# Row sums of four heads in one pass of TensorE, their quotients spread through DRAM, and two batches of x on chip instead of three

## The chip, the cores and the metric

The kernel runs on one NeuronCore of one Trainium2 chip. The metric is the device time of one execution in microseconds (us). Five engines work side by side, each through its own queue and in order: PE (TensorE) does matmuls, DVE (VectorE), ACT (ScalarE) and POOL (GpSimd) do elementwise work, SP (SyncE) issues the DMAs. SBUF is the on-chip memory with 128 partitions; matmuls write into PSUM. Everything is computed in float32.

## The reference, cut to what matters

x has 4 batches of 512 channels and 32 x 32 = 1024 positions. Four layers follow each other: softmax attention with 8 heads of 64 channels (layer 0), a linear attention (layer 1), softmax attention with one head of 512 (layer 2), and softmax attention with 4 heads of 128 (layer 3). The change is in layers 0 and 3, where each head does this:

```python
qkv = (xs @ Wp.T + bp).reshape(B, s, N_HEADS, 3 * D_K)
q, k, v = jnp.split(qkv, 3, axis=-1)
attn = jnp.einsum('bihd,bjhd->bijh', q, k) * SCALE
attn = jax.nn.softmax(attn, axis=2)
res = jnp.einsum('bijh,bjhd->bihd', attn, v)
...
out = res @ Wo.T + bo + xs
```

A softmax is a sum of exps over the keys for each query (the row sum), and a division by it. The kernel multiplies exp(scores) with v first, and divides the result.

## The kernel before, in words

`plain_path` is the program that runs (`general_path` is a fallback that this data doesn't take). Its loops run over the batches, layer by layer. PE's order is written out by hand (`manual_schedule` for PE); the order on the other engines comes from a planner that works with priorities and estimates. `later` holds work of PE that is due after a number of ticks (`tick`, once per step of attention or at chosen places of the projections); `pieces` holds parts of the next layer's work that fill `slot`s.

`attention` (L892) works on one batch. Queries are taken in two blocks qb of 512. The channels lie in four chunks g of 128: in layer 0 (`pair`) a chunk holds two heads of 64, in layer 3 one head. A step is (qb, g, i): in layer 0, i counts eight groups of 128 keys; in layer 3, four groups of 256 keys.

- `scores` (L908): PE multiplies keys with queries into a two-bank PSUM tile, four 64x64 matmuls that use the quarters of the array in layer 0, two full ones in layer 3. ACT takes the exp (L922) into one of four buffers `pt`, and DVE adds the pt of a chunk into `sum` (L926, L929), of which there are two buffers. In layer 3 a last add (L931) folds the two halves.
- `values` (L933), two steps behind: PE multiplies v with pt and accumulates over the keys into PSUM, one tile in layer 3, two (lower and upper half of the keys) in layer 0. There are four such tiles (`acc`). In layer 0, ACT copies the lower one to `ot` (L951) and DVE adds the upper one (L952).
- `sum_rows` (L961), once for each (qb, g): PE multiplies a matrix of ones with `sum`. This adds over the partitions and at once writes the total to every partition that needs it: one full matmul in layer 3 (L976), four on quarters of the array in layer 0 (L968), where ACT (L973) and DVE (L974) join two results. Then `invert` (L673) takes reciprocals on DVE (L675) and two maxima (L677, L678) for a test of the range at the end.
- `normalise` (L980): DVE multiplies the values with the reciprocals (L985), and ACT adds a bias to x (L988).
- `project_out` (L996), after the last chunk of a block: a first part and three further ones (`second`, `third`, `fourth`), with matmuls at L1018 and DVE adds at L1026 and L1048. They are due 2*per, and 2*per + 1, 2, 3 ticks later in layer 0 (per = 2), and 2*per and 2*per + 1, 1, 2 in layer 3 (per = 1).

So PE computes 32 units of row sums in layer 0 and 32 in layer 3. The tile `ot` is a single buffer.

x of a batch is 2 MB, 16 KB in each partition. Three of the four batches are on chip at a time (`x_tile`, L564). `away` (L568) stores a batch to DRAM and `back` (L572) fetches one. At the start batches 1 and 2 are loaded (L593); batch 3 follows when batch 0 has gone (L1596).

Of the kernel before, what the change touches and what calls it, by code (L numbers as in the profile page):

```python
# [13 lines left out]
F32 = mybir.dt.float32  # L14
AF = mybir.ActivationFunctionType
# [3 lines left out]
P = 128  # L19
B = 4  # L20
# [454 lines left out]
def plain_path(ctx: ExitStack, tc: tile.TileContext, d: dict, out: bass.AP, count):  # L475
# [35 lines left out]
    def sum_tile(name):  # L511
        return work.tile([P, 2, TB], F32, tag="sum", bufs=2, name=name)

    def v_tiles():

        return [work.tile([P, 2, C], F32, tag=f"v{i}", name=f"v{i}") for i in range(NT // 2)]
# [5 lines left out]
    def chunks_tile(tag, name, bufs=1):  # L522
        return work.tile([P, NC, TB], F32, tag=tag, bufs=bufs, name=name)
# [38 lines left out]
    xs, homes = {}, {}  # L562

    def x_tile(b):  # L564
        xs[b] = xpool.tile([P, NC, S], F32, tag="x", bufs=B - 1, name=f"x{b}")
        return xs[b]

    def away(b):  # L568
# [3 lines left out]
    def back(b):  # L572
        nc.sync.dma_start(x_tile(b), homes.pop(b))
# [15 lines left out]
    nc.sync.dma_start(wqkv0[:, :, 2 * C :], wview[:, :, 2 * C :])  # L589
    loaded0 = load_bias(d["bv0"], d["wo0n"], v_tiles()[:2])  # L590
    wo0 = load_wo(d["wo0"])
    for b in range(1, B - 1):
        nc.sync.dma_start(x_tile(b), xin[b])  # L593


    wv1 = chunks_tile("xn", "wv1", 2)
# [19 lines left out]
    nc.vector.memset(eps, 1e-5)  # L616
    UNITS = B * NTB * (NC + 1 + NC)
    tops = const.tile([P, 2, UNITS], F32, name="tops")
    unit = itertools.count()

    gmat = const.tile([P, P // GROUP, GROUP], F32, name="gmat")
# [51 lines left out]
    def invert(rd, ps):  # L673

        nc.vector.reciprocal(rd, ps)  # L675
        n = next(unit)
        nc.vector.tensor_reduce(tops[:, 0, n : n + 1], ps, AX.X, ALU.max)  # L677
        closing[:] = [nc.vector.tensor_reduce(tops[:, 1, n : n + 1], rd, AX.X, ALU.max).ins]  # L678

    def sum_inputs(tiles, inputs):  # L680

# [210 lines left out]
    def attention(b, q, key, v, heads, scale, wo, os, bo, hooks={}, last=False, end=None, plain=False):  # L892
# [12 lines left out]
        pts, accs, rds, outs, ots, exps = {}, {}, {}, {}, {}, []  # L905
        half = lambda i: slice(i * P // 2, (i + 1) * P // 2)

        def scores(n):  # L908
            qb, g, i = steps[n]
            ps = two_tile("sc")  # L910
            if pair:
                for h, s in itertools.product(range(2), range(2)):
                    nc.tensor.matmul(  # L913
                        ps[half(h), s, :], lhsT=key(g, i)[half(s), half(h)],
                        rhs=q[qb][half(s), g, :], start=True, stop=True,
                    )
# [5 lines left out]
            exps.append(nc.scalar.activation(pt, ps, AF.Exp, scale=scale).ins)  # L922
            pts[n] = pt
            if i == 1:
                accs[qb, g] = acc = sum_tile("sum")
                nc.vector.tensor_tensor(acc, pts[n - 1], pt, ALU.add)  # L926
            elif i > 1:
                acc = accs[qb, g]
                nc.vector.tensor_tensor(acc, acc, pt, ALU.add)  # L929
            if i == nsteps - 1 and not pair:  # L930
                nc.vector.tensor_tensor(acc[:, 0, :], acc[:, 0, :], acc[:, 1, :], ALU.add)  # L931

        def values(n):  # L933
            qb, g, i = steps[n]
            pt = pts.pop(n)
            if i == 0:
                outs[qb, g] = [acc_tile() for _ in range(2 if pair else 1)]
            if pair:

                for s, r in itertools.product(range(2), range(2)):  # L940
                    nc.tensor.matmul(  # L941
                        outs[qb, g][r][half(s), :],
                        lhsT=v[i // 2][half(r), i % 2, g * P + s * hd : g * P + (s + 1) * hd],
                        rhs=pt[half(r), s, :], start=(i == 0), stop=(i == NT - 1),
                    )
                if i == NT - 1:
                    if g == 0:
                        ots[qb] = chunks_tile("ot", "ot")
                    lower, upper = outs.pop((qb, g))
                    o = ots[qb][:, g, :]  # L950
                    nc.scalar.copy(o, lower)  # L951
                    nc.vector.tensor_tensor(o, o, upper, ALU.add)  # L952
                return
            for s in range(2):
                j = 2 * i + s
                nc.tensor.matmul(  # L956
                    outs[qb, g][0], lhsT=v[j // 2][:, j % 2, bass.ts(g, P)], rhs=pt[:, s, :],
                    start=(j == 0), stop=(j == NT - 1),
                )

        def sum_rows(qb, g):  # L961

# [14 lines left out]
            rds[qb, g] = row_tile("rd")  # L977
            invert(rds[qb, g], ps)

        def normalise(qb, g):  # L980
            rd = rds.pop((qb, g))
            if g == 0 and not pair:
                ots[qb] = chunks_tile("ot", "ot")
            o = ots[qb][:, g, :]
            nc.vector.tensor_tensor(o, o if pair else outs.pop((qb, g))[0], rd, ALU.mult)  # L985
# [111 lines left out]
        for m in range(0, len(steps) + 2, per):  # L1097
            for n in range(m, m + per):
                if n < len(steps):
                    scores(n)  # L1100
            for n in range(m, m + per):
                if n >= 2:
                    qb, g, i = steps[n - 2]
                    final = i == nsteps - 1

                    if final and not pair:
                        sum_rows(qb, g)
                    values(n - 2)
                    tick()
                    if final and pair:  # L1110
                        later.append([1, lambda qb=qb, g=g: (sum_rows(qb, g), normalise(qb, g))])
                    elif final:
                        normalise(qb, g)
                    if n - 2 == len(steps) - 1 and end is not None:
                        flush()
                        end_program(qb)
                    elif final and g == NC - 1 and plain and qb == NTB - 1:
                        later.append([2 * per + 1, lambda qb=qb: project_out_plain(qb)])
                    elif final and g == NC - 1:
                        rest = []  # L1120
# [344 lines left out]

    def layer_norm(b, tb, tiles):

        x = xs[b][:, :, bass.ts(tb, TB)]
        t = {}

        def add():
            s = t["s"] = row_tile("s")
            nc.vector.tensor_tensor(s, x[:, 0, :], x[:, 1, :], ALU.add)
            for c in range(2, NC):
                nc.vector.tensor_tensor(s, s, x[:, c, :], ALU.add)

        def center():
            xn = tiles[tb]
            t["ps"] = two_tile("lnsums")
            mean = t["ps"][:, 0, :]  # L1480
            nc.tensor.matmul(mean, lhsT=ones, rhs=t["s"], start=True, stop=True)
            for c in range(NC):
                nc.vector.scalar_tensor_tensor(
                    xn[:, c, :], mean, -1.0 / C, x[:, c, :], ALU.mult, ALU.add
                )
# [75 lines left out]

    def verdict():

        assert next(unit) == UNITS
# [9 lines left out]
    with tc.manual_schedule(engines={mybir.EngineType.PE}):  # L1574
# [8 lines left out]
        for b in range(B):  # L1583
# [86 lines left out]
        for b in range(B):  # L1670
# [73 lines left out]
        for b in range(B):  # L1744
# [92 lines left out]
```

## Time and profile before

| | |
|---|---|
| runs (3) | median 2488.96 us, 2487.82 to 2489.7 |
| the profiled execution | 2487.56 us, its span (first to last instruction) 2485.8 us |
| granted TensorE clock | 0.999 of full speed |
| busy | PE 2468.6 us (99%), DVE 1679.0 (68%), ACT 705.0 (28%), POOL 253.6 (10%) |
| layer 0, attention of batch 0 (80 to 212 us) | PE 130.75 us of 132.00, DVE 117.24, ACT 75.71 |
| layer 3, attention of batch 0 (1697 to 1825 us) | PE 128.00 us of 128.00, DVE 86.20, ACT 41.06 |
| DMA | 72.47 MB, mean 29 GB/s |

In a row of a group of instructions stand the line, the engine, the operation, output<-inputs, for PE the rows and columns of the array in use (64*64), the shape, the count, and then busy us, the mean ns of one, and the idle time of the engine before it with what ended it. A float32 matmul shows as two records. Records of PE overlap[...]; what a matmul costs is the time from its start to the next start. A row of waits gives the waiting engine, tile and line, what it waited for, the us in total, the times, and the longest. Rows of a timeline give start and length in us. A row of DMA issues gives the tile, the count, the KB of each and the median time from issue to landing.

### The profile page before, as it was taken

Reading aid. Unit: us, or ns where it says so; the run is one execution under the profiler, and the core shown is the slowest. Engines: PE = TensorE matmul, PEld = TensorE weight load, DVE = VectorE, ACT = ScalarE, POOL = GpSimd, SP = SyncE. Lnnn points to the kernel's source line nnn. Section 1 sums busy time; section 2 is a strip of 40 time slices with the busy share of each in tenths; the row PEclk is TensorE's granted clock in tenths of the full one; section 3 lists DMA queues with packets and bytes.
Section 4 is the critical chain, followed back from the end, with each engine's and each line's share of the span. In section 5 each row is a group of like instructions: output and inputs, shape, how many; then the busy total and the mean of one; then the engine's idle time right before and its main releaser. Section 6 shows DMA issues by size and latency. Waiting matters only on the chain.

```text
span 2485.8 us, 24942 instructions
## 1 busy us (share of the span) xinstructions
PE 2468.6 (99%) x10218; PEld 1277.3 (51%) x10218; DVE 1679.0 (68%) x1941; ACT 705.0 (28%) x863; POOL 253.6 (10%) x240
## 2 busy tenths in 40 slices
PE   9999999999999999999999999999999999999999
PEld 4545544554455444544645546445556446555653
DVE  3788588858875888647486775755664773665465
ACT  1454154315531544221211201112211320321121
POOL 4001100110011001201203021021010001002000
PEclk9999999999999999999999999999999999999999
DMA  5000010001000301010101010110010000000000
GB/s 216 1 1 1 5 69 1 1 5 69 1 1 5 119 10 51 0 72 9 59 0 68 5 67 19 51 68 17 17 51 1 5 13 17 1 17 17 1 9 27
DMA packets 23304, 72.47 MB, mean 29 GB/s; under 512 B 1808, under 2 KB 9488, under 8 KB 21136
## 3 DMA queue, kind: packets, MB, share of 16 engines
q1 hardware_dynamic: 23184, 70.82, 7.8%
q8 instruction: 82, 1.34, 0.2%
q14 instruction: 38, 0.31, 0.0%
HBM read 44.60 MB, written 25.17 MB: 28 GB/s over the span
## 4 chain that ended last, share of the span: by engine, by line
PE 96%; DVE 3%; issue 1%; ACT 0%; DMA 0%; SPq 0%; DVEq 0%
PE acc L703 20%; PE acc L824 11%; PE sc L918 9%; PE acc L956 9%; PE sc L913 8%; PE acc L941 8%; PE acc L831 8%; PE acc L1018 6%; PE acc L1232 6%; PE acc L1193 2%; PE acc L968 1%; PE acc L976 1%; PE feat L638 1%; DVE sum L929 1%; PE acc L638 1%; DVE rd L675 1%
## 5 line engine op out<-in xcount | busy, mean ns | idle before, releaser
L922 ACT ACTIVATE pt<-sc 128x1024 f32<-128x1024 f32 x384 | 380.3, 1022 | 650.4 <-PE sc L918 391.5
L929 DVE TENSOR_TENSOR sum<-sum,pt 128x1024 f32<-128x1024 f32 x256 | 313.9, 1226 | 45.8 <-ACT pt L922 34.4
L941 PE MATMUL acc<-pt,v 64*64 64x512 f32 x2048 | 291.0, 590 | 0.0
L913 PE MATMUL sc<-q,k 64*64 64x512 f32 x2048 | 273.7, 591 | 1.1 <-ACT pt L922 1.1
L956 PE MATMUL acc<-pt,v 128*128 128x512 f32 x512 | 239.9, 592 | 0.0
L918 PE MATMUL sc<-q,k 128*128 128x512 f32 x512 | 239.8, 593 | 0.0
L675 DVE RECIPROCAL rd<-acc 128x512 f32<-128x512 f32 x32 | 107.4, 3357 | 107.0 <-PE acc L976 107.0
L691 POOL TENSOR_TENSOR ws<-wqkv 128x256 f32<-128x256 f32 (+1 forms) x40 | 40.6, 1015 | 1334.8 <-PE acc L968 552.3
L703 PE MATMUL acc<-t,ws 128*128 128x512 f32 x384 | 173.9, 593 | 0.0
L941 PEld LDWEIGHTS acc<-pt,v 64*64 64x64 f32 x2048 | 104.2, 133 | 121.3 <-issue 98.3
L913 PEld LDWEIGHTS sc<-q,k 64*64 64x64 f32 x2048 | 101.1, 133 | 123.6 <-issue 92.4
L956 PEld LDWEIGHTS acc<-pt,v 128*128 128x128 f32 x512 | 97.3, 190 | 122.5 <-issue 120.5
L918 PEld LDWEIGHTS sc<-q,k 128*128 128x128 f32 x512 | 96.8, 190 | 112.8 <-issue 88.1
L703 PEld LDWEIGHTS acc<-t,ws 128*128 128x128 f32 x384 | 72.5, 190 | 86.6 <-issue 85.1
L675 DVE RECIPROCAL rd<-rs 128x512 f32<-128x512 f32 x32 | 107.3, 3352 | 1.1
L926 DVE TENSOR_TENSOR sum<-pt 128x1024 f32<-128x1024 f32 x64 | 76.7, 1198 | 42.1 <-ACT pt L922 42.1
L742 ACT COPY v<-acc 128x512 f32<-128x512 f32 x24 | 14.0, 585 | 287.9 <-PE acc L824 287.9
L824 PE MATMUL acc<-ws,t 128*128 128x256 f32 x384 | 87.3, 379 | 0.0
L831 PE MATMUL acc<-qs,w 128*128 128x512 f32 x192 | 86.6, 593 | 0.0
L831 PE MATMUL acc<-q,ln 128*128 128x512 f32 x192 | 85.8, 593 | 0.0
L733 DVE TENSOR_TENSOR v<-acc,v 128x512 f32<-128x512 f32 x72 | 49.4, 688 | 51.9 <-PE acc L824 51.7
L742 ACT COPY q<-acc 128x512 f32<-128x512 f32 x40 | 23.4, 585 | 207.8 <-PE acc L703 207.8
(318 smaller groups left out, 3698.2 us busy)
## 6 DMA issues: line engine op xcount, KB each, us to landing
home<-x SPq DMA_DIRECT2D x8, 2048.0 KB, 6.3
x<-home SPq DMA_DIRECT2D x8, 2048.0 KB, 7.8
out<-x SPq DMA_DIRECT2D x32, 256.0 KB, 2.1
x<-in_x SPq DMA_DIRECT2D x3, 2048.0 KB, 16.9
wo<-in_wo SPq DMA_DIRECT2D x3, 1024.0 KB, 5.3
w<-in_w SPq DMA_DIRECT2D x1, 3072.0 KB, 17.8
wqkv<-in_wqkv SPq DMA_DIRECT2D x1, 3072.0 KB, 10.1
wqkv<-in_wqkv SPq DMA_DIRECT2D x2, 1024.0 KB, 9.2
```

The costliest lines, as they stand in the source:

```text
L675: nc.vector.reciprocal(rd, ps)
L703: nc.tensor.matmul(ps, lhsT=w[:, m, :], rhs=x[:, m, :], start=start, stop=stop, skip_group_check=True)
L824: nc.tensor.matmul(ps[:, bass.ts(r, C // 2)], lhsT=x[:, m, bass.ts(2 * o + r, P)], rhs=w[:, m, :], start=(start and r == 0), stop=stop, sk ...
L831: nc.tensor.matmul(ps, lhsT=x[:, m, bass.ts(o, P)], rhs=w[:, m, :], start=start, stop=stop, skip_group_check=True,)
L913: nc.tensor.matmul(ps[half(h), s, :], lhsT=key(g, i)[half(s), half(h)], rhs=q[qb][half(s), g, :], start=True, stop=True,)
L918: nc.tensor.matmul(ps[:, s, :], lhsT=key(g, 2 * i + s), rhs=q[qb][:, g, :], start=True, stop=True)
L922: exps.append(nc.scalar.activation(pt, ps, AF.Exp, scale=scale).ins)
L929: nc.vector.tensor_tensor(acc, acc, pt, ALU.add)
L941: nc.tensor.matmul(outs[qb, g][r][half(s), :], lhsT=v[i // 2][half(r), i % 2, g * P + s * hd : g * P + (s + 1) * hd], rhs=pt[half(r), s, : ...
L956: nc.tensor.matmul(outs[qb, g][0], lhsT=v[j // 2][:, j % 2, bass.ts(g, P)], rhs=pt[:, s, :], start=(j == 0), stop=(j == NT - 1),)
L1018: nc.tensor.matmul(ps[i][:, bass.ts(o, n)], lhsT=w[:, m, bass.ts(o, P)], rhs=t[:, m, :], start=(start and m + o == 0), stop=(stop and m == ...
L1232: nc.tensor.matmul(ps[i, o], lhsT=w[m][:, bass.ts(o, P)], rhs=t[m], start=(start and m == 0), stop=(stop and m == 3), skip_group_check=True,)
```

## The change

In layer 0 the row sums of two chunks (four heads) become one unit, except for the last two chunks of the second query block, which stay with `sum_rows`. In layer 3 the four heads of the first query block, and the first three of the second, become one unit each; the last head stays with `sum_rows`. A unit (`sum_shared`) multiplies ones of 32 columns with each head's sum, and writes head k to partitions 32k to 32k + 31 of one PSUM tile. One `invert` serves the unit. As the reciprocals of a head are then on 32 partitions only, one row of each head is stored to DRAM, and loaded back broadcast to the partitions that need it; `normalise` of all chunks of the unit follows that. In layer 3, ACT copies the values out of PSUM to `ot` at the end of a chunk. `project_out` is due later where it follows a unit. The exps get a high priority in the planner. To make room for the new tiles, two batches of x are on chip instead of three, and `away`, `back` and the loads are put in another order. `tops` is set to zero at the start.

```diff
+    def many_tile(name):
+        return work.tile([P, NC, TB], F32, tag="many", name=name)
...
-        xs[b] = xpool.tile([P, NC, S], F32, tag="x", bufs=B - 1, name=f"x{b}")
+        xs[b] = xpool.tile([P, NC, S], F32, tag="x", bufs=2, name=f"x{b}")
...
-    for b in range(1, B - 1):
-        nc.sync.dma_start(x_tile(b), xin[b])
+    nc.sync.dma_start(x_tile(1), xin[1])
...
+    nc.vector.memset(tops, 0.0)
...
     def attention(...):
+        if pair:
+            shared = [[(qb, g), (qb, g + 1)] for qb in range(NTB) for g in range(0, NC, 2)][:-1]
+        else:
+            shared = [[(qb, g) for g in range(NC - qb)] for qb in range(NTB)]
+        group_of = {u: us for us in shared for u in us}
...
-            exps.append(nc.scalar.activation(pt, ps, AF.Exp, scale=scale).ins)
+            with soon():
+                exps.append(nc.scalar.activation(pt, ps, AF.Exp, scale=scale).ins)
...
-                accs[qb, g] = acc = sum_tile("sum")
+                acc = many_tile("sum")[:, :2, :] if pair and g % 2 and us else sum_tile("sum")
+                accs[qb, g] = acc
...
+            if i == nsteps - 1:
+                if g == 0:
+                    ots[qb] = chunks_tile("ot", "ot")
+                if (qb, g) in group_of:
+                    nc.scalar.copy(ots[qb][:, g, :], outs.pop((qb, g))[0])
...
+        def sum_shared(us):
+            heads = [(u, s) for u in us for s in range(2 if pair else 1)]
+            n = P // 4
+            ps = acc_tile()
+            for k, (u, s) in enumerate(heads):
+                acc = accs[u]
+                nc.tensor.matmul(
+                    ps[k * n : (k + 1) * n, :], lhsT=ones[:, :n],
+                    rhs=acc[:, s, :] if pair else acc, start=True, stop=True,
+                )
+            m = len(heads) * n
+            rd = row_tile("rd")
+            invert(rd[:m], ps[:m])
+            spread = work.tile([P, NC, TB], F32, tag="rds", name="rds")
+            home = dram.tile(
+                [len(heads), TB], F32, tag=f"quotients{len(heads)}", bufs=2, name="quotients"
+            )
+            nc.sync.dma_start(home, rd[0:m:n])
+            for s in range(2 if pair else 1):
+                to = spread[half(s) if pair else slice(0, P)]
+                nc.sync.dma_start(
+                    to[:, : len(us), :],
+                    home[s :: 2 if pair else 1].partition_broadcast(to.shape[0]),
+                )
+            for i, u in enumerate(us):
+                accs.pop(u)
+                rds[u] = spread[:, i, :]
+            return us
...
-                    if final and not pair:
+                    us = group_of.get((qb, g))
+                    closes = us and (qb, g) == us[-1]
+                    if final and not pair and closes:
+                        sum_shared(us)
+                    elif final and not pair and not us:
                         sum_rows(qb, g)
                     values(n - 2)
                     tick()
-                    if final and pair:
+                    if final and pair and closes:
+                        later.append(
+                            [1, lambda us=us: [normalise(*u) for u in sum_shared(us)]]
+                        )
+                    elif final and pair and not us:
                         later.append([1, lambda qb=qb, g=g: (sum_rows(qb, g), normalise(qb, g))])
-                    elif final:
+                    elif final and closes:
+                        for u in us:
+                            normalise(*u)
+                    elif final and not pair and not us:
                         normalise(qb, g)
...
+                        lead, *others = (4, 5, 6, 7) if pair else (2, 3, 3, 4)
+                        wait = (1 if pair else 2) if us else 0
                         later.append(
-                            [2 * per, lambda qb=qb, rest=rest: rest.extend(project_out(qb))]
+                            [lead + wait, lambda qb=qb, rest=rest: rest.extend(project_out(qb))]
                         )
-                        for i in (1, 2, 3) if pair else (1, 1, 2):
-                            later.append([2 * per + i, lambda rest=rest: rest.pop(0)()])
+                        for i in others:
+                            later.append([i + wait, lambda rest=rest: rest.pop(0)()])
...
-                if b == 1:
-                    nc.sync.dma_start(x_tile(B - 1), xin[B - 1])
+                if b + 1 < B:
+                    nc.sync.dma_start(x_tile(b + 1), xin[b + 1])
                 else:
-                    back(b - 2)
+                    back(0)
...
-                pieces.append(lambda: (away(B - 1), back(2)))
+                pieces.append(lambda: (away(B - 1), back(1)))
...
-            back((b + 3) % B)
+            back((b + 2) % B)
...
-            if b == 1:
-                xs.pop(0)
-                back(B - 1)
+            if 0 < b < B - 1:
+                xs.pop(b - 1)
+                back(b + 1)
```

More of the change, by code (lines that the diff above doesn't have):

```diff
@@ L675, in invert @@
         nc.vector.reciprocal(rd, ps)
-        n = next(unit)
-        nc.vector.tensor_reduce(tops[:, 0, n : n + 1], ps, AX.X, ALU.max)
-        closing[:] = [nc.vector.tensor_reduce(tops[:, 1, n : n + 1], rd, AX.X, ALU.max).ins]
+        n, m = next(unit), rd.shape[0]
+        for i, t in enumerate((ps, rd)):
+            closing[:] = [nc.vector.tensor_reduce(tops[:m, i, n : n + 1], t, AX.X, ALU.max).ins]
     def sum_inputs(tiles, inputs):
@@ L906, in attention @@
         half = lambda i: slice(i * P // 2, (i + 1) * P // 2)
+        if pair:
[3 more added lines that the diff above has]
+        group_of = {u: us for us in shared for u in us}
+        parts_of = {}
         def scores(n):
@@ L921, in scores @@
             pt = pt_tile("pt")
-            exps.append(nc.scalar.activation(pt, ps, AF.Exp, scale=scale).ins)
+            with soon():
+                exps.append(nc.scalar.activation(pt, ps, AF.Exp, scale=scale).ins)
             pts[n] = pt
+            us = group_of.get((qb, g), [])
             if i == 1:
-                accs[qb, g] = acc = sum_tile("sum")
+                acc = many_tile("sum")[:, :2, :] if pair and g % 2 and us else sum_tile("sum")
+                accs[qb, g] = acc
                 nc.vector.tensor_tensor(acc, pts[n - 1], pt, ALU.add)
@@ L930, in scores @@
             if i == nsteps - 1 and not pair:
-                nc.vector.tensor_tensor(acc[:, 0, :], acc[:, 0, :], acc[:, 1, :], ALU.add)
+                total = acc[:, 0, :]
+                if us:
+                    if g == 0:
+                        parts_of[qb] = many_tile("sums")
+                    total = accs[qb, g] = parts_of[qb][:, g, :]
+                nc.vector.tensor_tensor(total, acc[:, 0, :], acc[:, 1, :], ALU.add)
         def values(n):
@@ L959, in values @@
                 )
+            if i == nsteps - 1:
+                if g == 0:
+                    ots[qb] = chunks_tile("ot", "ot")
+                if (qb, g) in group_of:
+                    nc.scalar.copy(ots[qb][:, g, :], outs.pop((qb, g))[0])
         def sum_rows(qb, g):
@@ L978, in sum_rows @@
             invert(rds[qb, g], ps)
+        def sum_shared(us):
[26 more added lines that the diff above has]
+            return us
         def normalise(qb, g):
             rd = rds.pop((qb, g))
-            if g == 0 and not pair:
-                ots[qb] = chunks_tile("ot", "ot")
             o = ots[qb][:, g, :]
-            nc.vector.tensor_tensor(o, o if pair else outs.pop((qb, g))[0], rd, ALU.mult)
+            source = outs.pop((qb, g))[0] if (qb, g) in outs else o
+            nc.vector.tensor_tensor(o, source, rd, ALU.mult)
             xv = x[:, g, bass.ts(qb, TB)]
@@ L1466, in layer_norm @@
     def layer_norm(b, tb, tiles):
-        x = xs[b][:, :, bass.ts(tb, TB)]
+        x = lambda c: xs[b][:, c, bass.ts(tb, TB)]
         t = {}
@@ L1472, in add @@
             s = t["s"] = row_tile("s")
-            nc.vector.tensor_tensor(s, x[:, 0, :], x[:, 1, :], ALU.add)
+            nc.vector.tensor_tensor(s, x(0), x(1), ALU.add)
             for c in range(2, NC):
-                nc.vector.tensor_tensor(s, s, x[:, c, :], ALU.add)
+                nc.vector.tensor_tensor(s, s, x(c), ALU.add)
         def center():
@@ L1483, in center @@
                 nc.vector.scalar_tensor_tensor(
-                    xn[:, c, :], mean, -1.0 / C, x[:, c, :], ALU.mult, ALU.add
+                    xn[:, c, :], mean, -1.0 / C, x(c), ALU.mult, ALU.add
                 )
@@ L1562, in verdict @@
     def verdict():
-        assert next(unit) == UNITS
+        assert next(unit) <= UNITS
         ok = const.tile([P, 2 * UNITS], F32, name="ok")
```

## The prediction, as put on record before the change had run

> **What bounds the kernel now.** I read the page's part 1 first, then the list of waits of PE, then PE's groups, then its timeline. Part 1:
>
> ```profile
> span 2485.8 us, 24942 instructions
> ## 1 busy us (share of the span) xinstructions
> PE 2468.6 (99%) x10218; PEld 1277.3 (51%) x10218; DVE 1679.0 (68%) x1941; ACT 705.0 (28%) x863; POOL 253.6 (10%) x240
> ```
>
> PE is busy for 99% of the span; the chain that ended last gives PE 96%. So time is won only by taking work or waits off PE. The waits are small, and these four rows (us in total, times, longest) are what matters of them here:
>
> ```profile
> PE acc L1018 <- DVE x L1026: 2.9, 4, 0.7
> PE acc L968 <- DVE ot L952: 1.2, 4, 0.6
> PE sc L913 <- ACT pt L922: 1.1, 4, 0.3
> PE acc L1067 <- DVE ot L985: 0.8, 1, 0.8
> ```
>
> The row sums are two groups of PE (count | busy us, mean ns):
>
> ```profile
> L968 PE MATMUL acc<-sum,ones 64*64 64x512 f32 x256 | 47.5, 604 | 1.3 <-DVE ot L952 1.2
> ...
> L976 PE MATMUL acc<-sum,ones 128*128 128x512 f32 x64 | 32.7, 592 | 0.0
> ```
>
> One fp32 matmul is two records, so L968 is 32 units of 8 records (one per head pair and query block, layer 0), L976 is 32 units of 2 (one per head and block, layer 3). A mean of 592 ns is not the price: records overlap. The price is from start to start, in the timeline (start, length):
>
> ```profile
> 97.24 1.04 PE L968 MATMUL acc<-sum,ones 64*64 64x512 f32 x8
> 98.10 1.04 PE L941 MATMUL acc<-pt,v 64*64 64x512 f32 x8
> ...
> 1711.21 1.02 PE L976 MATMUL acc<-sum,ones 128*128 128x512 f32 x2
> 1712.07 1.88 PE L956 MATMUL acc<-pt,v 128*128 128x512 f32 x4
> ```
>
> Both kinds cost 0.86 us: two full-array records at 0.43 us, or eight records on quarters of the array, four at a time. Adding up, over all matmuls of PE's timeline, what each start comes later than the one before it allows, the L968 units lose 8.6 us more (up to 0.7 us in one). The reason is the vector engine: in layer 0's attention (80 to 212 us) DVE is busy for 117.2 of 132.0 us, and a unit needs two PSUM buffers, one of which DVE (L952) frees.
>
> [...] a 128x64 shape is there:
>
> ```profile
> 281.90 1.88 PE L703 MATMUL acc<-t,ws 128*128 128x512 f32 x4
> 283.71 1.94 PE L1370 MATMUL acc<-v,kf 128*64 128x512 f32 x8
> 285.58 0.43 PE L1381 MATMUL ksum<-ones,kpart 128*128 128x64 f32 x2
> ```
>
> Eight records start within 1.87 us instead of 8 x 0.43 = 3.43: two column halves do run together with all 128 rows in use. [...] L703's four records should end their turn at 281.90 + 1.72 = 283.62, L1370 starts at 283.71, so 0.09 us on the way in; of the 1.87 us, 1.72 are the eight records in pairs, and the other 0.15 I read as 0.09 on the way out and 0.05 inside. [...] nothing here shows four columns. [...]
>
> **The change part by part.**
>
> (a) Removed from PE. Layer 0: of 8 units per batch six go, 4 x 6 x 0.859 = 20.6 us. Layer 3: seven of 8 go, 4 x 7 x 0.859 = 24.1 us. The stalls of the removed layer 0 units: 24/32 of 8.6 = 6.4 us; the shared unit takes one PSUM buffer that ACT frees, and DVE sheds work (below). Together 51.1 us.
>
> (b) Added to PE: 3 shared units per batch in layer 0, 2 in layer 3, 20 in all. Four matmuls of 32 columns are 8 records. If four columns run together, that is 0.859 + 0.09 + 0.09 + 0.05 = 1.10 us, 22.0 us in all. Bounds for one: 0.95[...] and 3.67 (one column after the other, 8 x 0.43 + 0.23). I take 1.10, since the trace shows two columns and two rows by two columns at full rate[...].
>
> (c) DVE: per batch 3 inverses fewer in layer 0 and 5 in layer 3 (3.35 + 0.63 + 0.67 = 4.65 us each), and in layer 0 six adds of L974 (0.68) fewer. That is 18 us of 117 in a layer 0 attention. Off the path by itself; it takes away the cause of the stalls in (a), and of the 2.9 us that L1018 waits (its third part, four times, behind a DVE that runs late; in the new order a pair of scores lies between the second and third part). I take 2.9 off.
>
> (d) The quotients' round trip, the new wait. From the end of the reciprocal: store of 4 x 512 (2.1, the row of the output stores), then two broadcast loads, issued 0.4 apart, about 2.9 (between the 2.1 and the 3.1 to 3.3 of the broadcast of a bias). Rows:
>
> ```profile
> out<-x SPq DMA_DIRECT2D x32, 256.0 KB, 2.1
> ...
> brows<-in_bq SPq DMA_DIRECT2D x1, 256.0 KB, 3.1
> brows<-in_bv SPq DMA_DIRECT2D x1, 256.0 KB, 3.3
> ```
>
> That makes 5.5 us. Count from T, the start of the shared unit on PE, in layer 0. DVE still has an add of a sum to do, so the reciprocal starts at T + 1.9, ends at T + 5.2, the quotients land at T + 10.7, and two products of 0.69 end at T + 12.1. In DVE's order the two products stand behind the two reductions and two more adds (ready at T + 7.2), so DVE stands still for about 3.5 us. Queued behind are the adds of the next two exps; exps need their pt buffers (four) again only at about T + 13 and later, so PE doesn't feel that. What does feel it is project_out's second part in query block 0, which reads heads 4 to 7. On PE it stands at T + 1.10 + 0.86 (values) + 1.72 + 1.72 + 1.72 (scores, values, scores) + 0.86 + 1.91 (first part[...]) + 0.86 = T + 10.8. It waits 1.3 us, once per batch: 4 x 1.3 = 5 us. Bounds 0 (trip of 4.2) to 10 (trip of 6.7). The other eight groups of layer 0 are followed by no early reader. In layer 3 the first part stands four steps of 3.43 us behind the unit, at about T + 16, and four products end by T + 14: nothing. SP issues these DMAs in order; ahead of them stand only x moves, bias loads and output stores that are issued 10 us or more earlier.
>
> (e) Exps with priority: PE's waits for exps are 1.1 us, at the start of each layer 0 attention where nothing else stands in ACT. Nothing. In layer 3 ACT gets 28 copies of 0.585; ACT is busy 41 of 128 us there. Nothing; if a copy came first, an exp would be 0.6 late against 3.43 per step. project_out of query block 0 moves one step later in layer 0, two in layer 3, and ot is a single buffer: ACT's copy of the next block's first heads into it waits for the fourth part. Behind the copy stand exps whose scores PE computes after that part anyway: nothing. The memset of tops lies in the 14 us that DVE waits for x at the start.
>
> (f) Two x on chip. Every load now follows the store that frees its buffer. In layer 2 that is 6.3 (home) + 7.8 (back) after the last update of x. From the trace: the stores start at 1179.02, 1330.50 and 1480.11, so loads land at about 1193.1, 1344.6 and 1495.3; the first DVE readers stand behind joins that end at 1194.7 and 1345.3, and at 1496.6: spare 1.6, 0.7 and 1.3 us. In layer 3 the load for batch 3 now meets the statistics as that at 1855.15 does, where DVE lost 0.99 us and PE nothing. A late load stalls DVE with joins behind it, and PE has four PSUM buffers of slack. I take 1 us, bounds 0 and 6. The load of batch 2 that leaves the start stood behind all that PE waits for there: nothing.
>
> Sum: -51.1 + 22.0 - 2.9 + 5 + 1 = -26 us. The profiled execution took 2487.56 us (span 2485.8 and 1.8 around it): 2461.6. The median of the runs, 2488.96, is 1.4 above it: **2463**. With the bounds of (d) and (f) and 0.95 to 1.15 us per unit, this case alone spans 2454 to 2474.
>
> **The rivals.**
> Two columns at a time: each unit 1.72 + 0.23 = 1.95, in all 39, sum -9, 2480. For it: the trace shows at most two streams through a row of the array[...].
> The round trip on the path: 2 us more than I count, felt at every layer 0 group through late adds and pt buffers: about 12 x 1.3 + 4 x 0.7 more, 2480. For it: DVE is 85% full there with the wait; against: (c).
> Slower: columns one after the other. 20 x 3.67 = 73, sum +26, 2514. It decides from 2.4 us per unit ((51 - 3)/20). For it: four weights with 128 rows in use are shown nowhere; against: L1370.
> No effect: a wait gives back all that PE sheds, 2488; it would need some 25 us at places where none is shown.
>
> **How the numbers follow.** Forecast 0.68, two columns 0.08, round trip 0.12, no effect 0.04, slower 0.08. The range 2454 to 2481 takes in the forecast's and most of the next two. A measurement of this kernel can tell about 0.2% (5 us) from no change. Faster 0.88, same 0.04, slower 0.08.
>
> **What would show it.** The new group of row sums, 32 columns wide: next start 0.9 to 1.15 us after its first if (b) is right, about 1.9 or 3.6 for the rivals. PE's busy time near 2440. In the waits of PE a row of project_out's matmul behind the product with quotients or a reduction of ot, some 5 us in 4 to 8 times; if (d) is too small, rows of scores or exps behind DVE's adds. The L968 group's successor with 8 units and hardly any stall. DVE idle before the products, ended by a DMA, 3 to 4 us each. I am wrong if the shared unit costs over 1.5 us, or PE waits over 15 us for DVE.

## The result, and the profile after

The changed kernel takes 2483.09 us (median of 15 runs, 2481.78 to 2487.9), the kernel before 2488.83 us beside it (15 runs, 2487.6 to 2489.7). The ratio is 0.9979, with an interval of 0.9971 to 0.9987. So it is faster, by 5.7 us, where 26 were forecast; 2483 lies 2 us above the range. The profiled execution took 2483.01 us, its span is 2481.2 us.

First the lines that answer to those of before. Part 1 of the page:

```profile
span 2481.2 us, 24717 instructions
## 1 busy us (share of the span) xinstructions
PE 2449.9 (99%) x10122; PEld 1222.9 (49%) x10122; DVE 1530.0 (62%) x1822; ACT 708.9 (29%) x867; POOL 252.5 (10%) x240
```

PE has shed 96 records and only 18.7 us of busy time, DVE 149 us. The groups of row sums (count | busy us, mean ns | idle us before them) and the shared unit in PE's timeline (start, length):

```profile
L992 PE MATMUL acc<-sum,ones 64*64 64x512 f32 x64 | 13.7, 651 | 7.2 <-DVE sum L943 4.8 <-DVE ot L971 2.4
L1011 PE MATMUL acc<-sum,ones 128*32 128x512 f32 x96 | 12.8, 605 | 0.0
L1011 PE MATMUL acc<-sums,ones 128*32 128x512 f32 x56 | 8.5, 605 | 0.0
```

```profile
141.42 1.07 PE L1011 MATMUL acc<-sum,ones 128*32 128x512 f32 x8
142.42 1.09 PE L960 MATMUL acc<-pt,v 64*64 64x512 f32 x8
```

From the start of the unit to the next start is 1.00 us, where its 8 records one after the other would take about 3.4 (8 x 0.43). So four columns do run together. But the 8 units of layer 0 that are still summed one by one (L992) now wait 7.2 us. The waits of PE (us in total, times, longest) say for what:

```profile
PE acc L1072 <- DVE ot L1039: 7.5, 4, 2.0
PE acc L992 <- DVE sum L943: 4.8, 4, 1.4
...
PE sc L924 <- ACT pt L934: 3.5, 8, 0.6
PE acc L992 <- DVE ot L971: 2.4, 4, 0.6
PE acc L1072 <- DVE oi L687: 1.1, 4, 0.3
```

L1072 is the projection, L924 are scores of layer 0, L1039 is the product with the quotients, L943 the running add, L971 the add that joins the two halves of the values. All five rows lie in layer 0's attention and sum to 19.3 us; the corresponding rows of before came to 5.2. What stands behind them shows in DVE's timeline, here for the first shared unit (in brackets the idle time before an instruction, and what ended it):

```profile
113.81 3.35 DVE L678 RECIPROCAL rd<-acc 128x512 f32<-128x512 f32 x1
117.08 0.63 DVE L681 TENSOR_REDUCE tops<-acc 128x1 f32<-128x512 f32 x1
117.62 0.67 DVE L681 TENSOR_REDUCE tops<-rd 128x1 f32<-128x512 f32 x1
118.21 2.55 DVE L943 TENSOR_TENSOR sum<-sum,pt 128x1024 f32<-128x1024 f32 x2
123.91 1.29 DVE L1039 TENSOR_TENSOR ot<-ot,rds 128x512 f32<-128x512 f32 x2 [3.15 <-DMA rds<-quotients]
125.12 1.22 DVE L943 TENSOR_TENSOR sum<-sum,pt 128x1024 f32<-128x1024 f32 x1
```

The two products stand in DVE's queue behind two adds. DVE is through with the adds at 120.8 and stands still for 3.15 us until the loads land; the list of DVE's waits has this 12 times in layer 0, 37.2 us in all. The trip, from the end of the reciprocal (117.16) to the products (123.91), is 6.75 us, not 5.5. SP's queue splits it:

```profile
117.19 0.68 SPq L1023 DMA_DIRECT2D quotients<-rd  x1
119.00 1.32 SPq L1026 DMA_DIRECT2D rds<-quotients  x2
```

The loads are issued 1.8 us after the store, and from there it takes 4.9 us until DVE starts.

### The profile page after: what moved, and what is told of

The parts are those of the page before. It is cut to its first block, busy times and chain, and to the rows that moved or that the text cites. A ratio compares the mean times of both kernels' runs of the same rounds, so it can differ in the third digit from the quotient of the medians.

```text
span 2481.2 us, 24717 instructions
## 1 busy us (share of the span) xinstructions
PE 2449.9 (99%) x10122; PEld 1222.9 (49%) x10122; DVE 1530.0 (62%) x1822; ACT 708.9 (29%) x867; POOL 252.5 (10%) x240
## 4 chain that ended last, share of the span: by engine, by line
PE 90%; DVE 5%; DMA 3%; ACT 1%; issue 1%; SPq 0%; DVEq 0%; ACTq 0%
PE acc L706 20%; PE acc L827 11%; PE acc L975 9%; PE sc L929 9%; PE acc L834 8%; PE acc L1072 6%; PE acc L1300 6%; PE sc L924 6%; PE acc L960 5%; PE acc L1261 2%; DVE sum L943 2%; DMA rds<-quotients 2%; DVE rd L678 2%; PE feat L641 1%; ACT pt L934 1%; PE acc L641 1%
## 5 line engine op out<-in xcount | busy, mean ns | idle before, releaser
L943 DVE TENSOR_TENSOR sum<-sum,pt 128x1024 f32<-128x1024 f32 x256 | 314.4, 1228 | 149.3 <-ACT pt L934 139.0
L960 PE MATMUL acc<-pt,v 64*64 64x512 f32 x2048 | 260.1, 594 | 0.0
L924 PE MATMUL sc<-q,k 64*64 64x512 f32 x2048 | 254.1, 595 | 3.5 <-ACT pt L934 3.5
L924 PEld LDWEIGHTS sc<-q,k 64*64 64x64 f32 x2048 | 78.8, 134 | 147.6 <-issue 130.4
L960 PEld LDWEIGHTS acc<-pt,v 64*64 64x64 f32 x2048 | 79.7, 133 | 143.5 <-issue 140.4
L678 DVE RECIPROCAL rd<-acc 128x512 f32<-128x512 f32 (+1 forms) x24 | 80.5, 3353 | 39.2 <-PE acc L1011 39.2
L1072 PE MATMUL acc<-ot,wo 128*128 128x256 f32 x336 | 80.5, 382 | 7.5 <-DVE ot L1039 7.5
L1072 PEld LDWEIGHTS acc<-ot,wo 128*128 128x128 f32 x336 | 62.8, 190 | 38.2 <-issue 23.5
```

The costliest lines, as they stand in the source:

```text
L924: nc.tensor.matmul(ps[half(h), s, :], lhsT=key(g, i)[half(s), half(h)], rhs=q[qb][half(s), g, :], start=True, stop=True,)
L960: nc.tensor.matmul(outs[qb, g][r][half(s), :], lhsT=v[i // 2][half(r), i % 2, g * P + s * hd : g * P + (s + 1) * hd], rhs=pt[half(r), s, : ...
L1072: nc.tensor.matmul(ps[i][:, bass.ts(o, n)], lhsT=w[:, m, bass.ts(o, P)], rhs=t[:, m, :], start=(start and m + o == 0), stop=(stop and m == ...
```

## The experiments

All runs were timed beside the kernel before (medians 2488.2 to 2488.7 us in the three sets). The theories that the expectations name: **A**, in layer 0 DVE stands still until the quotients land, and what is queued behind the products comes late to PE. **B**, two batches of x on chip. **C**, the shared unit itself. **D**, the transfers of the trip disturb something, waited for or not. And step (d) of the prediction: of the trips only the one ahead of a projection is felt.

| label | us, median | range |
|---|---|---|
| e1_layer3_only | 2474.19 | 2473.66 to 2474.53 |
| e2_layer0_only | 2494.63 | 2491.52 to 2497.45 |
| e3_no_trip | 2454.11 | 2453.33 to 2454.84 |
| e5_two_x | 2487.87 | 2486.91 to 2488.84 |
| e3b_trip_unread | 2454.09 | 2453.58 to 2455.76 |
| e8_trip_one_group | 2463.41 | 2462.81 to 2465.36 |
| e6_products_later | 2488.72 | 2487.46 to 2493.6 |
| e10_all_later | 2474.53 | 2471.71 to 2476.09 |
| e12_two_held | 2465.93 | 2465.64 to 2467.99 |
| e13_all_held | 2455.35 | 2455.11 to 2456.07 |
| e7_two_hops | 2501.97 | 2500.36 to 2503.31 |
| e4_no_priority | 2481.68 | 2479.33 to 2483.54 |

### Which part: layer 3 alone, layer 0 alone, x alone

The first leaves layer 0's row sums as before, the second layer 3's; the third is the kernel before with the edits to x alone.

```diff
         if pair:
-            shared = [[(qb, g), (qb, g + 1)] for qb in range(NTB) for g in range(0, NC, 2)][:-1]
+            shared = []
```

```diff
         else:
-            shared = [[(qb, g) for g in range(NC - qb)] for qb in range(NTB)]
+            shared = []
```

e1_layer3_only:

> The changed kernel with layer 0 as it was before (row sums by sum_rows, no round trip there); layer 3 and x as changed. Theory A (in layer 0, DVE stands still for the quotients' round trip, and what is queued behind it holds PE): layer 3 has no such early reader, so it keeps its gain: 28 units of 0.86 us go, 8 of 1.07 us come, -15.5 us, 2473 us against 2489 before, with no wait of PE for a product with quotients. Theory B (two x on chip, with more loads close to their readers, cost what is missing): those 20 us stay lost here too, about 2490 us. Theory C (something in the shared unit itself, also in layer 3): gains shrink to 4 us or so, 2485 us.

e2_layer0_only:

> The changed kernel with layer 3 as it was before (sum_rows for each head); layer 0 and x as changed. Theory A: layer 0 alone costs more than it saves; the changed kernel's 2483 us plus the 15.5 us that layer 3 saved, 2498 us, slower than before by 0.4%. PE waits for the product with quotients 7 to 8 us in layer 0 and for sums 7 us, as in the changed kernel. Theory C: half the loss goes with the units, about 2486 us.

e5_two_x:

> The kernel before with one part of the change alone: two batches of x on chip, with the changed order of stores and loads. Theory A: within 1 us of before, 2488 to 2490 us. Theory B: slower by 10 to 20 us, 2500 us or more, with DVE waiting for x<-home and PE behind it.

Measured: 2474.19 (ratio 0.9944, 0.993 to 0.9957), 2494.63 (1.0025, 1.0015 to 1.0035) and 2487.87 (0.9999, 0.9991 to 1.0007). Layer 3's part gains 14 us, layer 0's part loses 6, and x costs nothing: B falls. C falls as well, as the same unit gains in layer 3. (For layer 0 alone A had named 2498 us, 3 us more than was measured.)

### Without the trip, and with the trip but nobody waiting

In e3_no_trip the products of layer 0 take the tile of reciprocals as it is:

```diff
             invert(rd[:m], ps[:m])
+            if pair:
+                for u in us:
+                    accs.pop(u)
+                    rds[u] = rd
+                return us
```

> The changed kernel, but in layer 0 the quotients of a shared unit are not spread: the store to DRAM and the two loads are left out, and the products multiply with the reciprocals as they stand on 4 times 32 partitions (this part of the computation is left out, so layer 0's quotients are not those of the reference). PE's work is the same. Theory A: DVE's idle time of about 3 us before each product goes, PE's waits for the products (7.5 us), for the sums of the last chunks (4.8 + 2.4 us) and for exps (3.5 us) go with it, 20 us or more in all: 2460 to 2464 us. Theory B or C: the waits stay, 2480 us or more.

In e3b_trip_unread the store and the loads are issued as in the change, but not read in layer 0:

```diff
-                rds[u] = spread[:, i, :]
+                rds[u] = rd if pair else spread[:, i, :]
```

> The change with its stores and loads of layer 0's quotients issued as they are, but the products of layer 0 take the unspread quotients, so that nothing waits for the loads (left out of the computation: the spreading of layer 0's quotients). Theory A, VectorE stands still until the loads land and what is queued behind it holds TensorE: no wait is left, 2452 to 2457 us, as without any trip. Theory D, the transfers themselves or their issue disturb something: they are still there, 2470 us or more.

Measured: 2454.11 (ratio 0.9862, 0.9847 to 0.9878) and 2454.09 (0.9866, 0.9851 to 0.9881). The transfers cost nothing, waiting for them costs 29 us: D falls, and A holds. That is more than the 20 or so (2460 to 2464 us for e3_no_trip) that I had put to A. Of the five rows of waits above only the first scores of each attention are left. This is the list of e3b, shown whole:

```profile
PE acc L706 <- DMA wqkv<-in_wqkv: 4.2, 1, 4.2
PE sc L924 <- ACT pt L934: 1.1, 4, 0.3
PE acc L1121 <- DVE ot L1039: 0.8, 1, 0.8
PE lnsums L1549 <- DVE s L1543: 0.7, 1, 0.7
```

### Which of the twelve trips

e8_trip_one_group keeps the trip only for chunks 2 and 3 of query block 0, the group with a projection behind it:

```diff
+            if pair and us[0][1] == 0:
+                for u in us:
+                    accs.pop(u)
+                    rds[u] = rd
+                return us
             spread = work.tile([P, NC, TB], F32, tag="rds", name="rds")
```

> The change with the trip through DRAM kept in layer 0 only for the group of chunks 2 and 3 of query block 0, the one with a projection close behind it (4 of the 12 groups); the other 8 take the unspread quotients (left out of the computation: the spreading of those). Step (d) of my prediction, that only this group has an early reader: it holds the whole 29 us that lay between no trip (2454) and the change (2483), 2478 to 2484 us. Theory A, each trip costs because VectorE stands still whoever reads: a third of the 29, that is 2461 to 2467 us.

Measured: 2463.41 (ratio 0.99, 0.9885 to 0.9915). The four groups that step (d) priced cost 9.3 us over no trip (2454.1), and the eight that it set to nothing cost the other 19.7. This is the run that breaks the prediction's step. Where the eight are felt can be read from PE's timeline, by the starts of the three shared units of a batch. First the change, then e3b, batch 0:

```profile
111.86 1.07 PE L1011 MATMUL acc<-sum,ones 128*32 128x512 f32 x8
...
141.42 1.07 PE L1011 MATMUL acc<-sum,ones 128*32 128x512 f32 x8
...
185.75 1.06 PE L1011 MATMUL acc<-sum,ones 128*32 128x512 f32 x8
```

```profile
110.96 1.06 PE L1011 MATMUL acc<-sum,ones 128*32 128x512 f32 x8
...
139.58 1.06 PE L1011 MATMUL acc<-sum,ones 128*32 128x512 f32 x8
...
181.72 1.07 PE L1011 MATMUL acc<-sum,ones 128*32 128x512 f32 x8
```

The first stretch is 29.56 against 28.62 us, the second 44.33 against 42.14. Done for all four batches, and for the third stretch up to the start of the last values of the attention:

| us lost to e3b, batches 0 to 3 | | | | | sum |
|---|---|---|---|---|---|
| after chunks 0, 1 of block 0 | 0.9 | 0.9 | 0.7 | 1.0 | 3.5 |
| after chunks 2, 3 of block 0 (projection) | 2.2 | 2.5 | 2.6 | 2.5 | 9.8 |
| after chunks 0, 1 of block 1 | 4.7 | 2.9 | 4.6 | 2.7 | 15.0 |

That is 28.3 of the 29 us. (The table is taken from one profiled execution of each kernel; 4 us or so of its third row come with a lower clock in batches 0 and 2, see the last section.) In the first row PE waits for exps: ACT can't start them, because the four pt buffers wait for DVE's late adds. ACT's timeline of the change:

```profile
126.43 1.03 ACT L934 ACTIVATE pt<-sc 128x1024 f32<-128x1024 f32 x1 [1.55 <-DVE sum L943]
```

In the third row the reader is `sum_rows` of the chunk after the group, here at 202 us:

```profile
199.67 1.04 PE L960 MATMUL acc<-pt,v 64*64 64x512 f32 x8
202.08 1.04 PE L992 MATMUL acc<-sum,ones 64*64 64x512 f32 x2 [1.38 <-DVE sum L943]
203.73 0.66 PE L992 MATMUL acc<-sum,ones 64*64 64x512 f32 x3 [0.60 <-DVE ot L971]
```

It reads the running sum, whose next adds stood behind the products from 194.6 to 199.0, and then a PSUM tile that DVE frees with L971, later still in the same queue.

### A longer trip

e7_two_hops puts a copy from DRAM to DRAM between the store and the loads, in layer 0:

```diff
             nc.sync.dma_start(home, rd[0:m:n])
+            if pair:
+                again = dram.tile([len(heads), TB], F32, tag="again", bufs=2, name="again")
+                nc.sync.dma_start(again, home)
+                home = again
```

> The change with a second hop from DRAM to DRAM between the store and the loads of layer 0's quotients, in all 12 groups. The store took 1.8 us from issue to the loads' issue, so the trip is about 2 us longer (estimate). Theory A: VectorE's 3.1 us wait becomes about 5 and TensorE feels 0.8 to 1 us of each further one, 12 x 2 x 0.9 = 22 us more, 2498 to 2512 us. If only the projection's wait counted: 4 x 2 = 8 us more, 2489 to 2493 us. If the trip's length doesn't matter: 2483 us.

Measured: 2501.97 (ratio 1.0053, 1.0039 to 1.0067), 19 us over the change. DVE's timeline has the first products at 125.89, after a reciprocal that ends at the same time as in the change: 2.0 us later.

```profile
125.89 1.29 DVE L1043 TENSOR_TENSOR ot<-ot,rds 128x512 f32<-128x512 f32 x2 [3.81 <-DMA rds<-again]
```

The time lies in the range that I gave for A, but that is in part luck, since the 19 us don't arise as A had it, 0.8 to 1 us from every further one in all 12 groups. The table above, made for e7 in the same way, has the sums 4.0, 24.8 and 20.0: of the 20 us that this execution is longer than the change's, 15 lie in the second row, at the projection, and 5 in the other eight groups together. The waits of PE show the same:

```profile
PE acc L1076 <- DVE ot L1043: 15.7, 4, 4.2
PE acc L992 <- DVE sum L943: 6.2, 4, 1.8
...
PE acc L992 <- DVE ot L971: 4.2, 4, 1.2
PE sc L924 <- ACT pt L934: 4.2, 8, 1.0
```

The wait for the products (L1076 here is the projection) grew by 8.2 us, four times the whole 2.0; the other rows together by 3. That makes 11 us. The rest agrees with the clock: in e7 TensorE's granted clock (0.993 over the whole span, 0.998 in the change) is 0.50 in seven stretches of layer 0, with PE busy for 28.1 us in them, in the change in two with 6.8 us. In the change, matmuls at that clock start 0.85 us apart instead of 0.43 (last section), so this is worth about 11 us more (an estimate from these figures). So the run shows that a longer trip costs more, and most where a projection reads the products; it gives no price for a further us of trip.

### Products later in DVE's queue

e6_products_later shares only chunks 0 and 1, and writes their products six steps later; e10_all_later shares all groups, with products six or four steps later, and moves the second and third part of the projection:

```diff
-                        later.append(
-                            [1, lambda us=us: [normalise(*u) for u in sum_shared(us)]]
-                        )
+                        later.append([1, lambda us=us: sum_shared(us)])
+                        to = 5 if g == NC - 1 else 7
+                        later.append([to, lambda us=us: [normalise(*u) for u in us]])
...
+                        if pair and us:
+                            others = [6, 7, 7]
                         for i in others:
```

(This is e10. In e6 the groups are those of chunks 0 and 1 alone, `for g in (0,)`; the products are due at 7 throughout, and the projection's last three lines are as in the change.)

> Layer 0 shares only the groups of chunks 0 and 1 (8 groups), and their products stand six steps of 1.72 us later in VectorE's queue than in the change, past the landing; chunks 2 and 3 are summed one by one as before. Against layer 3's part alone (2474), 16 units of 0.86 us on TensorE go and 8 of 1.10 come, 4.9 us. Theory A: the trips are hidden and VectorE's adds are not held, 2462 to 2468 us, with no VectorE wait for the loads. Theory D (transfers) or a cost in the units themselves: 2474 us or more.

> All 12 groups of layer 0 shared, products later in VectorE's queue: by six steps for chunks 0 and 1, by four for chunks 2 and 3, whose projection follows directly, with its second and third part a step later. Theory A: VectorE no longer stands still ahead of adds; what stays is the projection's own wait, some 2 us in each of 4 places with its consequences, so 2456 to 2464 us. Step (d) of my prediction, the projection's wait alone matters: it is not shortened much, 2475 us or more. Theory D: 2475 us or more as well.

Measured: 2488.72 (ratio 1.0003, 0.9995 to 1.0011) and 2474.53 (0.9944, 0.993 to 0.9957). Both miss what I expected, because the edit did not do what I wrote. The order of an engine's queue comes from the planner, and it set the products back behind two adds. (In e10 the first ones wait 3.01 us there.) So neither number speaks for D, which e3b has ruled out. DVE's timeline of e6:

```profile
118.21 2.55 DVE L943 TENSOR_TENSOR sum<-sum,pt 128x1024 f32<-128x1024 f32 x2
124.01 1.29 DVE L1039 TENSOR_TENSOR ot<-ot,rds 128x512 f32<-128x512 f32 x2 [3.26 <-DMA rds<-quotients]
```

In e6, moreover, both its groups in a batch are followed by a `sum_rows`, and its waits of PE for the running sum are 9.7 us in 8 times. e10 says something all the same: only the projection's parts moved, its wait for the products went from 7.5 to 0.2 us, and the time fell by 8.6 us against the change. Most of that is the second row of the table, which for e10 comes to 3.3 us instead of 9.8.

For the next two the products are tied behind the running add of the time when they are written (e12_two_held: chunks 0 and 1 only, the rest as in the change; e13_all_held: e10 with the tie):

```diff
+                adds.append(nc.vector.tensor_tensor(acc, acc, pt, ALU.add).ins)
...
-            nc.vector.tensor_tensor(o, source, rd, ALU.mult)
+            with tc.issue_after(adds[-1]) if pair else nullcontext():
+                nc.vector.tensor_tensor(o, source, rd, ALU.mult)
```

> The change with all its trips, but in layer 0 the products of chunks 0 and 1 (8 of the 12 groups) are tied on VectorE behind the running add of six steps later, so that five adds instead of two lie between the reductions and the products; chunks 2 and 3 stay as they are. (Writing them later alone had not moved them: the scheduler set them back behind two adds.) Theory A: the 8 groups no longer let VectorE stand still, and the time is that of the run whose 8 groups had no trip, 2461 to 2467 us. If the trips cost by anything else than standing still: 2478 us or more.

> All 12 groups' products tied behind a running add, six steps later for chunks 0 and 1, four for chunks 2 and 3, and the second and third parts of the projection behind them a step later (the version before, 2474.5, had the same but for the tie). Theory A: no VectorE wait for loads in front of adds, no late row sums, only the projection's own short waits, 2455 to 2461 us, faster than layer 3 alone (2474). If holding the products makes VectorE's backlog at the projection the new wait: 2470 us or more.

Measured: 2465.93 (ratio 0.9909, 0.9893 to 0.9924) and 2455.35 (0.9866, 0.9851 to 0.9881), both as A says. DVE's timeline of e13 has the same instructions, and no idle time ahead of the products:

```profile
117.90 5.20 DVE L943 TENSOR_TENSOR sum<-sum,pt 128x1024 f32<-128x1024 f32 x4
123.40 1.23 DVE L940 TENSOR_TENSOR sum<-pt 128x1024 f32<-128x1024 f32 x1 [0.30 <-ACT pt L934]
124.55 1.29 DVE L1040 TENSOR_TENSOR ot<-ot,rds 128x512 f32<-128x512 f32 x2
```

The trip is as long as it was. Five adds now lie ahead of the products and need 6.4 us, and the products start 7.7 us after the end of the reciprocal, 0.95 us later than in the change. What is behind them is on time all the same, since nothing stood still ahead of it: over layer 0 DVE's waits for the loads fall from 37.2 us in 12 times to 2.8 in 4. This version leaves nothing out; it is 33 us faster than the kernel before and 28 faster than the change, and lies 1.2 us above the kernel without the trip.

### The exps' priority

e4_no_priority:

```diff
-            with soon():
-                exps.append(nc.scalar.activation(pt, ps, AF.Exp, scale=scale).ins)
+            exps.append(nc.scalar.activation(pt, ps, AF.Exp, scale=scale).ins)
```

> The change without the priority of the exps. Step (e) of my prediction, the priority is worth nothing: 2481 to 2486 us. If the priority saves part of TensorE's waits for exps (3.5 us in the change): 2486 to 2492 us; if it does harm by putting exps ahead of the copies that free TensorE's accumulators: 2478 us or less.

Measured: 2481.68 (ratio 0.9973, 0.9962 to 0.9983); the change's own interval of 0.9971 to 0.9987 overlaps with it. The priority can't be told from nothing.

## Why the prediction was wrong, by its steps

**(d), the quotients' round trip: wrong, and all of the miss.** Without (d) the forecast was 2463 - 5 = 2458; the kernel without the trip took 2454. With the trip it took 2483, so (d) is 29 us instead of 5, and 24 - 4 is the 20 us by which the forecast was off. Two things in (d) failed, and they are not of the same weight.

The size of the trip: 6.75 us for 5.5, since from the issue of the loads to the products it took 4.9 us and not 3.3. For this my own bound was there, "10 (trip of 6.7)", and the four groups ahead of a projection cost 9.3. That DVE's stall came out near the forecast, 3.15 us for 3.5, is luck: from the end of the reciprocal the two reductions and the two adds take 3.6 us (117.16 to 120.76), so after T + 5.2 DVE would have been free at T + 8.8 and not at T + 7.2, and with quotients at T + 10.7 the stall would have been 1.9 us.

The reasoning on what stands behind DVE's wait is the step that broke: "so PE doesn't feel that" and "the other eight groups of layer 0 are followed by no early reader". I had named the adds queued behind the products and checked only whether the next exps lack a buffer. I didn't follow the queue on. Even for the exps my own figures were too tight: with products up to T + 12.1 an add of 1.2 us behind them ends at T + 13.3, after the T + 13 at which a buffer is needed. In the trace (T = 111.86) ACT has come to that exp at 124.88, T + 13.0, and the add ends at 126.34, T + 14.5. On the average DVE has room (in the change it is busy for 99 of the 132 us from 80 to 212), but the room comes in small pieces, and the delay of one stall was still there when the next `sum_rows` read the running sum and when a PSUM tile for it was to be freed. In block 0 PE did feel the pt buffers, by 0.9 us per group. The eight groups cost 18 to 20 us, where the prediction had nothing; some 4 of them came with the lower clock that followed two of the stalls.

The rival "round trip on the path", given 0.12, had the mechanism right (late adds and pt buffers, felt at every layer 0 group; the late row sums it did not name) and the size nearly: 18.4 us more than (d), 2480; measured 24 more.

**(a) and (b), row sums on PE: right.** Layer 3's part was 28 x 0.859 - 8 x 1.10 = 15.3 us, less 1 for x; measured 14.0. The unit takes 1.00 us to the next start, and the eight records ahead of it take 0.97 (140.45 to 141.42) instead of 0.86, so some 0.1 more. That four columns run together was my estimate, from the pairs of L1370; no row of before shows it. The rivals "two columns" and the slower "columns one after the other" fall with this line.

**(c), relief of DVE: right where the trip is away.** With e3's 2454.1 layer 0 alone gains 20.1 over e1; its steps (20.6 + 6.4 + 2.9 - 12 x 1.10) gave 16.7; no run here explains the other 3.4. The 7.2 us at L992 in the change show that this relief was then taken back by the trip.

**(e) and (f): right.** The priority and the two batches of x can't be told from nothing. In (f) that is e5; the loads in layer 2 and 3 leave no row in the waits of PE.

**The signs to look for.** The text said that PE's waits for DVE above 15 us would make it wrong: the four rows with DVE add to 15.8, and 3.5 for exps behind DVE's adds come on top.

## What to carry to other kernels

A wait in an in-order queue cost here what stood behind it (29 us), not what waited in it: list the instructions queued behind it and follow each to its readers, up to the point where the engine has caught up, before a stall on a lightly loaded engine is called free. A transfer that lands later than the place in the queue where the planner sets its reader was hidden here by tying the reader behind work that is at hand (products 1 us later gained 28 us, together with the projection's parts a step later); writing the reader later is not enough where a planner orders the queue. One part of a change can lose what another part wins (14 and -6 us here), so each is timed alone.

## What the runs showed of the hardware

After the stall of 1.38 and 0.60 us at 202 us the granted clock of TensorE fell to half for 3.41 us. The columns of this view of the change are the stretch, its length, then busy time and count of PE, PEld, DVE, ACT and POOL, the clock, and two on DMA:

```profile
200.83:204.24 3.41, 1.55 (x10) 0.43 (x14) 3.41 (x4) 2.12 (x3) 0.00 (x0) 1.00 0.02 5
204.24:207.65 3.41, 3.41 (x24) 1.05 (x20) 3.27 (x4) 0.59 (x1) 2.24 (x3) 0.50 0.00 0
```

Most matmul records in the second stretch last 1.01 to 1.06 us instead of 0.59, and they start in fours 0.85 us apart instead of 0.43. In the change this happens in batches 0 and 2 (at 204.24 and 699.17) and not in 1 and 3, and the third row of the table shows what it costs: 4.7 and 4.6 against 2.9 and 2.7 us, about 2 us each time. In the kernels without the trip or with all products held the granted clock over the whole span was 0.999 to 1.000, in the change's profiled execution 0.998. Each fall in layer 0 lasts 3.41 us or, twice in e7, 6.83; the two of the change start 494.93 us apart, which is 145.0 times 3.413. In the 3.41 us ahead of the fall at 204.24 PE was busy for 1.55 us and idle for 1.86, in two parts. So a PE stall of 2 us cost up to 4 here. That the stall causes the fall was not tested by itself, and which stalls are followed by one stays open: a stretch of the change with 1.62 us of idle time (from 398.80) was not followed by a fall, one of e7 with 1.46 (from 459.83) was.
